# A Fourier layer's first pass over 64 images: another list of steps with the x transform in seven products, and DRAM chunk rows 72 KB apart

## The chip, the core and the metric

The kernel runs on one core of a Trainium2 chip. The metric is device time in microseconds from start to end of one execution. The core has a matrix engine (PE, with its weight loads shown apart as PEld), a vector engine (DVE), a scalar engine (ACT), a general engine (POOL), a queue engine that issues DMAs (SP), and 16 DMA engines between DRAM and the on-chip memory. PE writes its results into PSUM only, and ACT or DVE read them from there. Each engine works through its own instructions in order and waits on semaphores for the others.

## The reference, cut to what matters

Four Fourier layers run on 64 images of 256 x 256 points and 32 channels; then a small transformer block follows. Everything is fp32.

```python
v = transpose(concat([x, gx, gy]) @ p_w + p_b)        # 64 images, 32 channels, 256 x 256
for i in range(4):
    x_ft = rfft2(v)                                     # only 24 x 12 modes are used
    out_ft[:, :, :12, :12]  = einsum('bixy,ioxy->boxy', x_ft[:, :, :12, :12], W1[i])
    out_ft[:, :, -12:, :12] = einsum('bixy,ioxy->boxy', x_ft[:, :, -12:, :12], W2[i])
    v = irfft2(out_ft) + einsum('bcxy,cd->bdxy', v, w_w[i]) + w_b[i]
    v = (v - mean(v)) * rsqrt(var(v) + 1e-5) * bn_g[i] + bn_b[i]   # over batch and image
    if i < 3: v = relu(v)
h = concat([v @ q_w + q_b, txt])                        # 256 + 77 rows of 256 per image
h = h + attention(layernorm(h))
h = h + top_half_ffn(layernorm(h))
```

## The kernel before

**Stages.** The work of the Fourier layers is regrouped into passes over all images. `forward_first` takes the modes of the input, `mix` multiplies the modes by the layer's weights and yields the scale `s_` and shift `t_` of the normalization, and `layer(i, ...)` is one pass over the 64 images. It makes the activated image of layer i (inverse transform plus channel product, relu), writes it to DRAM for the next pass, and takes its forward transform and its sum of squares, which the next `mix` needs. There are three such passes (i = 0, 1, 2; "first", "second" and "third pass" here) and then the transformer stage, which reads the last image tensor (`ch<-v`).

**An image in a pass.** An image is cut into 8 chunks t. On chip a chunk is a tile `vo` of 128 partitions x 8 rows x 256 points; four `vo` buffers are used in turn. In DRAM an image is a tensor `vd`, 128 rows (partitions) of 8 chunks of 8 x 256 fp32, so one chunk of one row is 8 KB in one piece. There are two sets of 64 such tensors, which the passes read and write by turns.

**Steps.** The order of the work in a pass is a list of words written out by hand, `ORDER[0]` for the first pass and `ORDER[1]` for the second and third. The pass goes through the list once per image b; a word `name@n` acts on image b + n, and a suffix `.a` or `.d` picks ACT or DVE. What the words do, with the line that issues the work:

| word | engine | what it does |
|---|---|---|
| `lx`, `am`, `ld` | POOL, SP (and POOL), SP | load input rows (L649), load the mixed modes (L634) and scale them on POOL (L642), load a chunk of the last pass (L667, not in the first pass) |
| `sp`, `spT` | PE L673, DVE L681 | inverse transform over x for half an image; transpose it into tile `y` |
| `pre` t | PE L693 (and L704 after the first pass) | inverse transform over y plus channel product of chunk t |
| `evA`, `evB` | ACT L716 or DVE L718 | relu of one half of `pre` t from PSUM into `vo` |
| `st` t | SP L724, L728 | store chunk t to `vd`: in the first pass two DMAs of 512 KB, later one of 1 MB |
| `turn` t | DVE L733 | transpose chunk t into `t32` |
| `prod` t | PE L754 (L745 with `.w`) | channel product of chunk t for the next layer's squares |
| `sqA`, `sqB` | ACT L765 | square one half of it, with the sum kept |
| `y` k | PE L776 | forward transform over y, part k of 8, summed in PSUM |
| `half`, `zt0`, `zt1` | ACT L786, DVE L794 | move one half of the y result out of PSUM; transpose both into `zt` |
| `x`, `xe`, `xt`, `xo`, `xs` | PE, DVE or ACT, PE, ACT, SP | forward transform over x and its way to DRAM |

**The x transform has two forms.** The line `turned = "xt" in ORDER[min(i, 1)]` chooses. Where the list has no `xt`, as in the first pass before, `x` makes 12 products with the data stationary and the table of 96 columns moving (L819), and `xo` reads the result. Where it has `xt`, as in the second and third pass, `x` makes 4 products with the table `FX` stationary (64 columns) and 384 data columns moving (L808), `xe` copies the result out of PSUM (L831, L833), and `xt` makes 3 products that turn it and add its two halves (L838).

**The ring.** PSUM is cut into four slots of two banks. `pre`, `prod` and `y` take two slots each, `sp` and `x` one. A slot is taken in program order, always the one that has been free longest, and the step waits on the chip until whoever read the slot last is done:

```python
mine = sorted((k for k in range(4) if free[k] >= 0), key=lambda k: free[k])[:n]
```

A slot comes free (`close`) with `evA`/`evB` for `pre`, with `sqA`/`sqB` for `prod`, with `spT` for `sp`, with `zt0` and `half` for `y`, and with `xo` for `x`. While the eight `y` parts of one image are summed, two of the four slots are held, and everything else passes through the other two. Which slot a step gets thus follows from the list alone, and so does what each engine meets in which order.

**DMA queues.** All stores, chunk loads and `am` loads stand on SP's queue in the order of the list; `lx` and the scaling of `am` stand on POOL.

Of the kernel before, what the change touches and what calls it, by code (L numbers as in the profile page):

```python
# [9 lines left out]
F32 = mybir.dt.float32  # L10
# [6 lines left out]
S = 256  # L17
# [17 lines left out]
def _tables():  # L35
# [90 lines left out]


ORDER = [(
    "spT1 pre2 sqB1 lx0@1 evA2.a st1 evB2.d st2 pre3 evA3.d evB3.a prod0 y0@-1 sqB0 st0 "
    "sqA0 y1@-1 prod2 y2@-1 sqA2 turn0 am@2 sqB2 lx1@1 turn1 turn2 y3@-1 pre6 evB6.d "  # L130
    "y4@-1 y5@-1 evA6.a turn3 prod3 sqB3 y6@-1 y7@-1 sqA3 pre4 half.a@-1 st6 zt0@-1 lx2@1 "
    "evB4.a pre5 evA4.d prod4 evA5.a evB5.a turn4 sqA4 st3 sqB4 sp0@1 spT0@1 zt1@-1 turn5 "
    "st5 pre7 evB7.a lx3@1 evA7.a prod5 sqB5 prod6 sqA6 st4 x@-1 sqB6 turn6 sqA5 pre1@1 "
    "st7 xo@-1 pre0@1 evA1.a@1 evB1.d@1 evB0.a@1 xs@-2 evA0.d@1 prod7 sqB7 turn7 sqA7 "
    "prod1@1 sp1@1 sqA1@1 "
), (
    "evA2.a@1 evB2.a@1 ld5 ld7 pre4 ld0@1 turn6 prod6 evA4.a x@-1 evB4.d xe.d@-1 turn4 "
    "sqA6 sqB6 prod4 xt@-1 st2@1 turn2@1 sqA4 pre5 sqB4 xo@-1 am@2 evA5.d evB5.a pre3@1 "
# [15 lines left out]
def tile_fno_fusion_transformer(ctx: ExitStack, tc: tile.TileContext, a, cst_d, grid_d, out):  # L154
    nc = tc.nc
    x = a["x"].rearrange("b x y o -> b x (y o)")
    B = x.shape[0]
# [4 lines left out]
    dram = ctx.enter_context(tc.tile_pool(name="dram", bufs=1, space=DRAM))  # L162
# [19 lines left out]
    epsc = const.tile([128, 1], F32, name="epsc")  # L182
    nc.vector.memset(epsc, EPS)

    vd = [dram.tile([128, 8, 8, S], F32, name=f"v{b}_{n}") for n in range(2) for b in range(B)]
    vd = [vd[:B], vd[B:]]
    mix_d = [dram.tile([2, M, 2, B, 32 * C], F32, name=f"mix{i}") for i in range(L)]
    xh_d = [dram.tile([128, B, 144], F32, name=f"xh{i}") for i in range(1, L)]
# [1099 lines left out]
```

## Time and profile before

| what | value |
|---|---|
| median of 3 runs | 11210.26 us (11203.83 to 11220.63) |
| the profiled execution | 11214.0 us, of which span 11212.1 us, granted clock 0.984 |
| PE, PEld | 10666.4 us (95%), 5509.9 us (49%) |
| DVE, ACT, POOL | 8487.2 us (76%), 6483.7 us (58%), 1448.1 us (13%) |
| DMA | 3456.25 MB, mean 308 GB/s |
| `turn` on DVE (L733) | 1536 of 2292 ns |
| squares on ACT (L765) | 3072 of 1013 ns |
| evictions on ACT (L716), on DVE (L718) | 1792 of 1023 ns, 1280 of 1216 ns |
| x transform of the first pass (L819) | 1536 matmul records of 278 ns, from 264.6 to 2548.2 us |
| x transform of the second and third pass (L808, L838) | 1024 records of 499 ns, 768 of 281 ns; `xe` 128 of 557 ns |

The span is the time from the first to the last instruction on the core; the profiled execution is 1.9 us longer than its span. An fp32 product is recorded as two matmuls. A matmul's end is modelled, several run side by side in the array, and one that waits inside the array counts as busy: PE's 95% is therefore no measure of how full PE is, and its starts, in order of time, say more. "<-DMA v<-vo" after a time in brackets means that the engine stood idle for that time until a store had landed.

### The profile page before, as it was taken

What the parts mean: (1) busy time and instruction counts of PE and PEld (TensorE: products, weight loads), DVE (VectorE), ACT (ScalarE), POOL (GpSimd) and SP (SyncE); (2) the same over time, 40 slices, a digit from 0 to 9 for tenths busy, and PEclk for the clock granted to TensorE, in tenths of its full rate; (3) what the DMA queues carried; (4) which work ended last, traced back from release to release, by engine and by line L of the source; (5) the groups of instructions that cost most, each with busy time, mean ns of one, the idle gap of its engine ahead of it and who ended that gap; (6) DMA issues with size and microseconds to landing.
All of it is one profiled execution on the core that took longest, in us unless ns stands there. A gap on an engine that the chain in (4) does not pass through costs nothing. (4 is left out here: it accounts for less than half of the span.)

```text
span 11212.1 us, 395184 instructions
## 1 busy us (share of the span) xinstructions
PE 10666.4 (95%) x177174; PEld 5509.9 (49%) x177174; DVE 8487.2 (76%) x10525; ACT 6483.7 (58%) x10673; POOL 1448.1 (13%) x2179
## 2 busy tenths in 40 slices
PE   6999999997999999999799999999997999999999
PEld 3555555553444444444334444444443666666666
DVE  6888888887777777777777777777776666666665
ACT  5777777775665666666556566656663333333333
POOL 1111111110000000000000000000000333333333
PEclk8999999999999999999999999999998999999999
DMA  6767766678999999999899999999997555555553
GB/s 211 248 244 250 248 245 248 247 248 321 377 385 385 379 383 386 389 380 385 316 358 389 380 385 378 390 386 381 386 386 293 227 226 226 226 226 226 226 227 136
DMA packets 676795, 3456.25 MB, mean 308 GB/s; under 512 B 116248, under 2 KB 165784, under 8 KB 346008
## 3 DMA queue, kind: packets, MB, share of 16 engines
q1 hardware_dynamic: 609664, 3366.67, 76.6%
q0 software_dynamic: 58288, 60.60, 2.3%
q8 instruction: 1386, 22.71, 0.8%
q10 hardware_dynamic: 7144, 3.72, 0.1%
q14 instruction: 313, 2.56, 0.1%
HBM read 1733.60 MB, written 1696.92 MB: 306 GB/s over the span
## 5 line engine op out<-in xcount | busy, mean ns | idle before, releaser
L765 ACT ACTIVATE ring<-ring 128x1024 f32<-128x1024 f32 x3072 | 3112.4, 1013 | 1093.9 <-PE ring L745 612.9
L733 DVE STREAM_TRANSPOSE t<-vo 128x2048 f32<-128x2048 f32 x1536 | 3482.9, 2292 | 33.2 <-ACT vo L716 12.2
L716 ACT ACTIVATE vo<-ring 128x1024 f32<-128x1024 f32 x1792 | 1800.6, 1023 | 1584.1 <-PE ring L704 1264.5
L776 PE MATMUL ring<-t,cst 32*32 32x512 f32 x49152 | 1996.3, 599 | 34.5 <-issue 28.5
L754 PE MATMUL ring<-vo,w 32*32 32x512 f32 x40960 | 1898.8, 601 | 21.0 <-ACT vo L716 19.3
L718 DVE TENSOR_SCALAR vo<-ring 128x1024 f32<-128x1024 f32 x1280 | 1546.6, 1216 | 451.7 <-PE ring L704 276.5
L693 PE MATMUL ring<-cst,y 24*128 24x256 f32 x16384 | 1307.6, 404 | 89.3 <-ACT vo L716 45.5
L776 PEld LDWEIGHTS ring<-t,cst 32*32 32x32 f32 x49152 | 853.0, 103 | 979.5 <-issue 615.2
L642 POOL TENSOR_TENSOR ams<-ams,bns 48x512 f32<-48x512 f32 x384 | 401.1, 1044 | 6880.5 <-DMA ams<-mix 5410.8
L693 PEld LDWEIGHTS ring<-cst,y 24*128 24x128 f32 x16384 | 834.7, 185 | 922.5 <-ACT ring L765 246.5
L704 PE MATMUL ring<-vin,ws 32*32 32x512 f32 x32768 | 1196.2, 604 | 0.5 <-issue 0.5
L754 PEld LDWEIGHTS ring<-vo,w 32*32 32x32 f32 x40960 | 648.2, 103 | 845.5 <-issue 441.1
L681 DVE STREAM_TRANSPOSE y<-ring 128x1024 f32<-128x1024 f32 x384 | 761.2, 1982 | 341.4 <-PE ring L673 340.3
L794 DVE STREAM_TRANSPOSE zt<-ring 128x1024 f32<-128x1024 f32 x192 | 374.9, 1953 | 687.2 <-PE ring L776 687.2
L693 PE MATMUL ring<-mv,y 29*128 29x256 f32 x8192 | 704.2, 403 | 36.4 <-ACT ring L765 19.4
L693 PEld LDWEIGHTS ring<-mv,y 29*128 29x128 f32 x8192 | 455.8, 185 | 369.1 <-ACT ring L765 209.7
L1237 POOL DMA_DIRECT2D out_dram<-o x1024 | 511.3, 508 | 665.4 <-DVE o L1232 622.7
L765 ACT ACTIVATION_READ_ACCUMULATOR ring<-ring 128x1 f32 x3072 | 583.9, 190 | 0.0
L745 PE MATMUL ring<-vo,w 64*64 64x512 f32 x4096 | 506.8, 603 | 1.4 <-issue 1.4
L673 PE MATMUL ring<-ams,cst 49*128 49x512 f32 (+1 forms) x1536 | 452.0, 641 | 58.6 <-POOL ams L642 34.4
L1036 PE MATMUL hp<-ch,win 128*32 128x512 f32 x4096 | 471.9, 601 | 5.1 <-DMA ch<-v 5.1
L704 PEld LDWEIGHTS ring<-vin,ws 32*32 32x32 f32 x32768 | 249.1, 103 | 351.9 <-issue 350.9
(384 smaller groups left out, 10233.5 us busy)
## 6 DMA issues: line engine op xcount, KB each, us to landing
vin<-v SPq DMA_DIRECT2D x1024, 1024.0 KB, 10.3
v<-vo SPq DMA_DIRECT2D x1024, 1024.0 KB, 10.0
v<-vo SPq DMA_DIRECT2D x1024, 512.0 KB, 5.2
ch<-v SPq DMA_DIRECT2D x512, 1024.0 KB, 12.6
mix<-ob SPq DMA_DIRECT2D x48, 1024.0 KB, 4.9
ams<-mix SPq DMA_DIRECT2D x384, 96.0 KB, 8.7
xin<-in_x_dram SPq DMA_DIRECT2D x16, 1024.0 KB, 8.8
mv<-in_x_dram POOLq DMA_DIRECT2D x256, 64.0 KB, 7.7
```

Of the source, the lines that this page charges most:

```text
L681: nc.vector.transpose(y_[b, h].rearrange("p q c -> p c q"), ring[key][0][1].rearrange("p n (c k) -> p (n c) k", k=32),)
L693: nc.tensor.matmul(ps[n][:, 256 * r:256 * r + 256], lhsT=y_[b, t // 4][32 * n:32 * n + K, q:q + 4, :].rearrange("p q c -> p (q c)"), rhs=m ...
L704: nc.tensor.matmul(ps[n][32 * j:32 * j + 32], lhsT=ws[32 * n:32 * n + 32], rhs=v[32 * n:32 * n + 32, 2 * j:2 * j + 2, :], start=False, sto ...
L716: nc.scalar.activation(to, ring[key][h][1], AF.Relu)
L718: nc.vector.tensor_scalar(to, ring[key][h][1], 0.0, None, ALU.max)
L733: nc.vector.transpose(t32[b, t // 2][:, :, 8 * (t % 2):8 * (t % 2) + 8, :].rearrange("p y s c -> p s y c"), vo[b, t].rearrange("p s (y l) ...
L745: nc.tensor.matmul(ps[j][64 * m:64 * m + 64], lhsT=w64[64 * n:64 * n + 64], rhs=vo[b, t][64 * n:64 * n + 64, 2 * j:2 * j + 2, :], start=Tr ...
L754: nc.tensor.matmul(ps[n][32 * j:32 * j + 32], lhsT=w4[i + 1][32 * n:32 * n + 32], rhs=vo[b, t][32 * n:32 * n + 32, 2 * j:2 * j + 2, :], st ...
L765: nc.scalar.activation(ps, ps, AF.Square, accum_out=acc[:, at:at + 1])
L776: nc.tensor.matmul(ps[n][32 * j:32 * j + 32], lhsT=FYT[32 * n:32 * n + 32, k, :], rhs=t32[b, j][32 * n:32 * n + 32, k].rearrange("p s c -> ...
L1036: nc.tensor.matmul(hp[32 * g:32 * g + 32], lhsT=win[:, 7 - t:39 - t], rhs=ch[:, g], start=False, stop=t == 7, skip_group_check=True,)
L1237: nc.gpsimd.dma_start(out[b, 64 * n + 16 * g:64 * n + 16 * g + 16].rearrange("(p t) d -> p t d", t=2), o[32 * g + 8 * n:32 * g + 8 * n + 8 ...
```

## The change

The list of the first pass is replaced as a whole; it now has `xe.d` and `xt`, so the first pass takes its x transform in the second form (4 + 3 products). Per image the list still has 8 `pre`, 8 `prod`, 8 `y`, 8 `turn`, 16 squares and 16 evictions; of the evictions 11 are on ACT and 5 on DVE, where it was 10 and 6. More of image b + 1 is now done in the round of image b (`pre2`, `prod0`, `prod1` with their evictions and squares). The list of the second and third pass stays.

In DRAM each `vd` row gets a ninth chunk, which is never written or read: the 128 rows of an image lie 72 KB apart where they were 64 KB apart, for every store of the three passes, every chunk load of the second and third, and the loads of the transformer stage.

```diff
 ORDER = [(
-    "spT1 pre2 sqB1 lx0@1 evA2.a st1 evB2.d st2 pre3 evA3.d evB3.a prod0 y0@-1 sqB0 st0 "
-    "sqA0 y1@-1 prod2 y2@-1 sqA2 turn0 am@2 sqB2 lx1@1 turn1 turn2 y3@-1 pre6 evB6.d "
-    "y4@-1 y5@-1 evA6.a turn3 prod3 sqB3 y6@-1 y7@-1 sqA3 pre4 half.a@-1 st6 zt0@-1 lx2@1 "
-    "evB4.a pre5 evA4.d prod4 evA5.a evB5.a turn4 sqA4 st3 sqB4 sp0@1 spT0@1 zt1@-1 turn5 "
-    "st5 pre7 evB7.a lx3@1 evA7.a prod5 sqB5 prod6 sqA6 st4 x@-1 sqB6 turn6 sqA5 pre1@1 "
-    "st7 xo@-1 pre0@1 evA1.a@1 evB1.d@1 evB0.a@1 xs@-2 evA0.d@1 prod7 sqB7 turn7 sqA7 "
-    "prod1@1 sp1@1 sqA1@1 "
+    "y0@-1 st0 y1@-1 lx0@1 sqB1 turn0 turn1 st7@-1 sqA1 pre3 y2@-1 y3@-1 lx1@1 st2 evA3.a "
+    "turn2 y4@-1 evB3.a pre6 y5@-1 evB6.d lx2@1 evA6.a st1 turn3 prod2 y6@-1 sqA2 sqB2 "
+    "y7@-1 lx3@1 pre4 zt0@-1 half.a@-1 evA4.a turn6 st3 prod3 st6 evB4.a sp0@1 sqA3 pre5 "
+    "sqB3 spT0@1 evA5.a evB5.a st4 prod4 pre0@1 sqA4 zt1@-1 evB0.d@1 x@-1 xe.d@-1 sqB4 "
+    "turn4 evA0.a@1 prod6 sqA6 xt@-1 sqB6 prod5 xo@-1 sqB5 pre7 st5 sqA5 turn5 evA7.d "
+    "am@2 evB7.a pre1@1 prod0@1 evB1.d@1 evA1.a@1 sqA0@1 prod7 sqB0@1 sp1@1 xs@-2 sqB7 "
+    "turn7 sqA7 pre2@1 spT1@1 evB2.d@1 prod1@1 evA2.a@1 "
 ), (
...
-    vd = [dram.tile([128, 8, 8, S], F32, name=f"v{b}_{n}") for n in range(2) for b in range(B)]
+    vd = [dram.tile([128, 9, 8, S], F32, name=f"v{b}_{n}") for n in range(2) for b in range(B)]
```

## The prediction

> **What bounds it now.** I read the busy times by stage first, then one image of the first pass in order of time, engine by engine, then the waits. Columns of the stages: length, busy us of PE, weight loads, DVE, ACT, POOL, granted clock, DMA share, GB/s.
>
> ```profile
> 110.00:2460.00 2350.00, 2232.23 (x42548) 1175.85 (x42548) 2073.55 (x1270) 1761.89 (x2783) 282.39 (x387) 0.98 0.69 245
> 2700.00:5420.00 2720.00, 2668.18 (x53760) 1147.33 (x53754) 2084.51 (x1215) 1665.30 (x2616) 127.59 (x122) 1.00 0.97 383
> 5640.00:8440.00 2800.00, 2742.43 (x55340) 1180.20 (x55317) 2145.39 (x1249) 1711.85 (x2688) 129.64 (x124) 1.00 0.97 383
> 8600.00:11212.00 2612.00, 2516.92 (x15296) 1749.67 (x15296) 1733.79 (x6201) 967.42 (x1980) 847.42 (x1472) 0.99 0.56 219
> ```
>
> The reader sees four stages: first pass, second, third, transformer. PE looks full in all, but its ends are modelled; DMA is nearly full in passes two and three alone. The new list acts on the first line, the new pitch on all four. One image of the first pass (start, us, engine, line, record count; an fp32 product is two records, so x16 is one `pre`, x32 one `prod` or one `y`, x24 the x transform):
>
> ```profile
> 1472.34 2.01 PE L693 MATMUL ring<-mv,y 29*128 29x256 f32 x32
> 1474.60 2.58 PE L754 MATMUL ring<-vo,w 32*32 32x512 f32 x64 [0.25 <-ACT vo L716]
> 1477.37 1.13 PE L673 MATMUL ring<-ams,cst 54*128 54x512 f32 x4 [0.20 <-ACT ring L765]
> ...
> 1488.90 1.16 PE L693 MATMUL ring<-mv,y 29*128 29x256 f32 x16
> 1490.00 2.31 PE L776 MATMUL ring<-t,cst 32*32 32x512 f32 x62
> ...
> 1498.68 1.15 PE L754 MATMUL ring<-vo,w 32*32 32x512 f32 x32
> 1499.76 1.13 PE L673 MATMUL ring<-ams,cst 54*128 54x512 f32 x4
> 1500.82 1.64 PE L693 MATMUL ring<-mv,y 29*128 29x256 f32 x16
> 1502.39 3.76 PE L754 MATMUL ring<-vo,w 32*32 32x512 f32 x64
> 1506.08 2.92 PE L819 MATMUL ring<-cst,zt 128*128 128x96 f32 x24
> 1508.93 1.36 PE L693 MATMUL ring<-mv,y 29*128 29x256 f32 x20
> ```
>
> The cadence is 1508.93 - 1472.34 = 36.6 us. What PE must do in it: 8 `pre` at 1.0, 8 `prod` at 1.1, 8 `y` at 1.1, 2 `sp` at 1.06, x 2.85: 30.6 us. DVE: 8 `turn` at 2.2, 2 `spT` at 1.9, 2 `zt` at 1.96, 6 evictions at 1.17: 32.3 us. So no engine is full. The pass is bound by a **chain through the ring**: four PSUM slots, each filled by PE and emptied by ACT or DVE before the next step may write.
>
> From the rows in order of time I take: slot free to PE 0.1; `prod` start to its first square 1.3; square 1.03; `pre` start to eviction 1.18 on ACT, 1.24 on DVE; eviction 0.95 and 1.17; `y` 1.12; `sp` start to `spT` 1.2. The old chain, from `pre1` of one image to `pre1` of the next: pre1, evB1.d 2.41; prod7 1.4; sqB7 1.03; sp1 1.3; spT1 1.9; evB2.d, evA3.d 2.4; y0, y1 2.34; prod2 1.3; sqA2, sqB2 2.06; pre6 1.1; y4, y5, prod3, y6, y7 5.6; zt0 1.96; rest of pre5 0.9; evA5, evB5 1.9; sqA4, sqB4 2.06; evB7, evA7 1.9; prod6 1.2; x 2.85. Sum 35.6. The image above has 36.6, and one more wait:
>
> ```profile
> 1503.02 1.94 ACT L716 ACTIVATE vo<-ring 128x1024 f32<-128x1024 f32 x2 [0.71 <-DMA v<-vo]
> ```
>
> evB7 waits until the store of chunk 3 has left its `vo` buffer (issued at 1492.8, landed at 1502.9 by the trace's landing events). 36.6 - 0.7 = 35.9 against the sum 35.6: the chain is the right one. The mean cadence of the pass is 36.5 (starts of the `half` copy), so such waits cost some 0.65 per image.
>
> **The x transform, with the list.** Removed: 12 products with the data stationary, 2.85 us. Added: what passes two and three already do,
>
> ```profile
> 4238.24 1.51 PE L808 MATMUL ring<-zt,cst 128*64 128x384 f32 x8
> 4240.75 0.87 PE L838 MATMUL ring<-id,xe 128*128 128x48 f32 x6
> ```
>
> 1.44 + 0.80 = 2.24 on PE, and a DVE copy between (`xe`, 0.56). PE saves 0.6 per image. That is 64 x 0.6 = 39 us only if PE is the bound, and it is not; but x was the chain's last link, so what counts is the new chain. One eviction moves from DVE to ACT (DVE -1.17 + 0.56, ACT +0.95); DVE ends near 31.7 and ACT near 28 of 36: no bound.
>
> **The new list.** I gave every step the slot that `take` gives it (the longest free first) and followed the last wait back from `pre7` to `pre7`: sqB5, sqA5 2.06; evB7 0.95; prod0 1.4; sqA0 1.03; sp1 1.3; spT1 1.9; prod1 1.4; sqB1, sqA1 2.06; pre3 1.1; y2, y3, y4 3.36; pre6 to evB6.d 1.24; evB6.d 1.17; prod2 1.2; y6, y7 2.3; zt0 1.96; prod3 1.2; sp0 1.2; spT0 1.9; prod4 1.4; sqA4 1.03; x 1.54; prod6 1.3; sqA6 1.03; prod5 1.4. Sum 36.4, against 35.6 by the same prices: **+0.8 per image**. The shorter x and its split are eaten by both `spT` (1.9 each, sp0's now ahead of prod4) and by evB6 ahead of prod2 standing in the chain.
>
> Stores: on SP's queue the order is now st0, st7, st2, st1, st3, st6, st4, st5, then the two `am` loads and `xs`. st1 stands behind st2, which waits for evA2, the last step of the list. Each `vo` buffer (four, in turn) is needed again by the fourth `pre` after it; by the times of my chain a store then has at least 13.7 us from the moment SP may issue it (st1, needed by evA4), where st3, held behind st6, has 11.1 now (needed by evB7). So the 0.65 of store waits should shrink. Ends: all of it stays, or all of it goes. I take half, -0.33, since a landing took 10 us and slow packets in the DMA engines move with the list. Net +0.43 x 64 = +28 us. The x loads on POOL (`lx`), issued earlier, have over 20 us of cover before pre0; `am` moves from early to late in the image and is needed one image later, at sp0: both nothing.
>
> A rule that speaks against the list: the Trainium skill, "TensorEngine Tiling (Array Packing)", Key Properties, says that changing the tiling mode drains the array. The list goes from 13 changes of tile shape per image to 19. Row: a lone `pre` between others takes 1.1 (1488.90 to 1490.00), a pair 2.0 to 2.1, so a change there and back costs some 0.1, and six more 0.3 at most. My prices already stand in such places, so I add nothing; by the rule alone it would be up to +19 us, kept for the range.
>
> **The pitch.** A chunk row of 8 KB lies 72 KB from its neighbour, not 64; all transfers keep their sizes and counts. The skill's "DMA: Bandwidth & Descriptors", Latency and other measured facts, gives 207 GB/s per direction at a pitch of 512 KiB and 214 when padded: at most 3.3%, and nothing is stated at 64 KiB. Row: the trace's packets of 8 KB in passes two and three have a median of 309 ns (16 engines: 424 GB/s) and a mean of 328; the excess sits in two bursts of each image, one read of chunk 0 (496 ns) and the first packets after an idle queue, while the other chunks of the same pitch run at 310 to 315. A pitch that hurt would slow them all. By the row: 0. By the rule: DMA is 97% full in 5520 us, 3.3% is 182 us, at most 164, as the shortest image of these passes took 43.35 and the mean is 44.65. Below nothing: a new pitch with 2% slower packets would fill the DMA and cost some 110 us. I take 0. In the transformer the chunk loads hide behind PE (DMA share 0.56).
>
> **Sum**: 11214 (profiled execution, span 11212.1) + 28 = 11242; the runs shown have their median 4 us below it: **11238 us**, 0.25% slower. 0.2% (22 us) is about what a measurement can tell from no change.
>
> **Rivals.** *Store waits go wholly*: +0.8 - 0.65 = +0.15, +10 us: no change. For it: the slack of 13.7 us; against: landings spread. *PE decides*: the 0.6 counts in full, -39 us, 11171; for it PE's 95%, against it the 30.6 of 36.6. *The pitch pays*: half of 182 us, with the list's +28: 11150; for it DMA at 97% and evictions that wait for stores there, against it the 310 ns. *Slower still*: store waits stay and the drains count, (0.8 + 0.3) x 64 = +70, 11280; or the pitch costs 110: 11348. *The edit does nothing*: the pass tests the list for "xt", so the seven products do come.
>
> **Chances**: forecast 0.35, slower still 0.10, no change 0.24, PE decides 0.15, pitch pays 0.16. Slower 0.45, same 0.24, faster 0.31. The range 11120 to 11340 leaves out a pitch that pays or costs in full; the forecast's own is 11228 to 11270.
>
> **What will show it.** First-pass cadence 36.9 (36.5 before), with ACT's waits for `v` stores halved; zt0 still idle before y7; L808 and L838 at 1.44 and 0.80 in the first pass; passes two and three at 44.65 per image and 8 KB packets at 309 ns. Wrong if the cadence is under 36.3, or if passes two and three move by over 0.3 per image.

## The result, and the profile after

| | before | after |
|---|---|---|
| median, 8 runs each | 11203.66 us (11192.29 to 11220.63) | 11234.68 us (11222.58 to 11247.84) |
| ratio, 95% interval | 1 | 1.0024 [1.0015, 1.0032] |
| span of the profiled execution, granted clock | 11212.1 us, 0.984 | 11239.3 us, 0.982 |
| first pass, one `mix` to the next | 2442.6 us | 2488.5 us |
| second and third pass | 2978.2 and 2974.9 us | 2965.4 and 2969.9 us |
| from the last `mix` to the end | 2699.7 us | 2701.5 us |

The change costs 31 us by the medians, and 27 us by the ratio and by the two profiles. All of the loss is in the first pass, +46 us; before the first `mix` 3 us are saved, and the other two passes are 18 us shorter in this one profile (the second experiment shows what that is worth). The same four stages of the kernel after (length, busy us of PE, weight loads, DVE, ACT, POOL, granted clock, DMA share, GB/s):

```profile
110.00:2460.00 2350.00, 2146.29 (x41260) 933.13 (x41262) 2005.34 (x1248) 1782.56 (x2797) 277.18 (x377) 0.98 0.69 241
2700.00:5420.00 2720.00, 2671.23 (x53904) 1150.27 (x53904) 2092.97 (x1220) 1665.81 (x2615) 127.39 (x122) 1.00 0.97 385
5640.00:8440.00 2800.00, 2742.44 (x55258) 1180.68 (x55254) 2142.88 (x1248) 1708.88 (x2683) 129.49 (x124) 1.00 0.97 383
8600.00:11212.00 2612.00, 2512.98 (x15251) 1745.03 (x15252) 1735.39 (x6216) 963.49 (x1972) 835.29 (x1455) 0.99 0.57 222
```

In 2350 us of the first pass PE, the weight loads and DVE are less busy than before at the same granted clock (0.98), ACT a little more: x is shorter, one eviction went from DVE to ACT, and fewer images fit into the stretch. So the pass got longer with less work for PE. The other three lines are nearly those of before. One image of the first pass after, PE in order of time:

```profile
1442.47 1.15 PE L754 MATMUL ring<-vo,w 32*32 32x512 f32 x32 [0.75 <-DVE zt L794]
1443.56 1.13 PE L673 MATMUL ring<-ams,cst 54*128 54x512 f32 x4
...
1449.24 1.51 PE L808 MATMUL ring<-zt,cst 128*64 128x384 f32 x8 [0.27 <-ACT ring L765]
1450.68 1.14 PE L754 MATMUL ring<-vo,w 32*32 32x512 f32 x32
1451.75 0.87 PE L838 MATMUL ring<-id,xe 128*128 128x48 f32 x6
1452.55 1.78 PE L754 MATMUL ring<-vo,w 32*32 32x512 f32 x32
...
1455.71 0.70 PE L693 MATMUL ring<-mv,y 29*128 29x256 f32 x4 [0.20 <-ACT ring L765]
...
1459.19 1.15 PE L754 MATMUL ring<-vo,w 32*32 32x512 f32 x32 [0.25 <-DVE vo L718]
1460.31 1.13 PE L673 MATMUL ring<-ams,cst 54*128 54x512 f32 x4
...
1467.10 1.15 PE L693 MATMUL ring<-mv,y 29*128 29x256 f32 x16
1468.18 3.40 PE L776 MATMUL ring<-t,cst 32*32 32x512 f32 x96
1471.51 1.15 PE L693 MATMUL ring<-mv,y 29*128 29x256 f32 x16
...
1474.03 1.15 PE L754 MATMUL ring<-vo,w 32*32 32x512 f32 x32 [0.26 <-DVE vo L718]
...
1479.44 1.14 PE L754 MATMUL ring<-vo,w 32*32 32x512 f32 x30 [0.74 <-DVE zt L794]
```

From prod3 to prod3 it is 1479.44 - 1442.47 = 36.97 us. PE waits at places that the forecast's chain names: prod3 (the first and the last row) for zt0, x for sqA4, prod2 (1474.03) for evB6 on DVE. prod7 (1459.19) waits for evB1 on DVE as well; that is no link of the forecast's chain, which goes through sqA0 to sp1 there.

**A better measure than the mean.** The starts of the `half` copies give one cadence per image (61 of them). Their 10th percentile is taken for the cadence of the list when nothing disturbs it, and is called the floor from here on; the mean less the floor is the disturbance. e1 to e10 are the experiments of the next section. The last column names the x transform and the list, old as in before, new as in after; the pitch is 64 KB where no other is named.

| kernel | ratio to before, 95% interval | floor | median | mean | x form, list |
|---|---|---|---|---|---|
| before | 1 | 36.08 | 36.42 | 36.53 | old, old |
| after | 1.0024 [1.0015, 1.0032] | 36.97 | 36.98 | 37.15 | new, new, 72 KB |
| e1 | 1.0032 [1.002, 1.0044] | 36.97 | 36.99 | 37.14 | new, new |
| e2 | 0.9994 [0.9988, 1.0] | 36.08 | 36.44 | 36.54 | old, old, 72 KB |
| e3 | 1.0096 [1.0076, 1.0116] | 38.38 | 38.4 | 38.52 | old, new |
| e4 | 1.0047 [1.0031, 1.0062] | 36.55 | 37.0 | 37.2 | new, old |
| e5 | 1.0011 [1.0002, 1.0019] | 36.2 | 36.52 | 36.62 | new, old, `xt` before `pre1` |
| e6 | 1.0000 [0.9992, 1.0008] | 36.07 | 36.28 | 36.57 | old, old, `st3` early |
| e7 | 0.9990 [0.9982, 0.9999] | 36.07 | 36.33 | 36.49 | e6 with 72 KB |
| e8 | 1.0006 [0.9997, 1.0014] | 36.58 | 36.59 | 36.73 | new, new, `pre6` early |
| e9 | 1.0002 [0.9994, 1.001] | 36.59 | 36.6 | 36.68 | e8 with 72 KB |
| e10 | 1.0106 [1.0091, 1.0122] | 37.88 | 37.97 | 38.56 | e9, `y6`, `y7` before `prod2` |

So the floor grew by 36.97 - 36.08 = 0.89 per image, and the disturbance shrank from 0.45 to 0.18. Over the 62 intervals before the last image that is +39 us; the last image, from its predecessor's `half` to `mix`, takes 45.7 us instead of 40.4 (+5), and the start 139.8 instead of 137.9 (+2): the 46 us.

### The profile page after: what moved, and what is told of

It reads as the page before. It is cut to its first block, busy times and chain, and to the rows that moved or that the text cites. A ratio compares the mean times of both kernels' runs of the same rounds, so it can differ in the third digit from the quotient of the medians.

```text
span 11239.3 us, 394221 instructions
## 1 busy us (share of the span) xinstructions
PE 10623.4 (95%) x176534; PEld 5285.2 (47%) x176534; DVE 8452.6 (75%) x10525; ACT 6536.9 (58%) x10737; POOL 1445.8 (13%) x2179
## 5 line engine op out<-in xcount | busy, mean ns | idle before, releaser
L716 ACT ACTIVATE vo<-ring 128x1024 f32<-128x1024 f32 x1856 | 1858.1, 1022 | 1601.1 <-PE ring L704 1266.2
L776 PE MATMUL ring<-t,cst 32*32 32x512 f32 x49152 | 1908.6, 599 | 48.0 <-issue 30.4
L754 PE MATMUL ring<-vo,w 32*32 32x512 f32 x40960 | 1812.5, 601 | 79.4 <-DVE zt L794 46.3
L718 DVE TENSOR_SCALAR vo<-ring 128x1024 f32<-128x1024 f32 x1216 | 1478.2, 1216 | 533.4 <-PE ring L704 278.8
L776 PEld LDWEIGHTS ring<-t,cst 32*32 32x32 f32 x49152 | 785.9, 103 | 1014.1 <-issue 683.4
L754 PEld LDWEIGHTS ring<-vo,w 32*32 32x32 f32 x40960 | 564.9, 103 | 892.0 <-issue 408.0
```

The lines of the kernel that those rows point to most:

```text
L716: nc.scalar.activation(to, ring[key][h][1], AF.Relu)
L718: nc.vector.tensor_scalar(to, ring[key][h][1], 0.0, None, ALU.max)
L754: nc.tensor.matmul(ps[n][32 * j:32 * j + 32], lhsT=w4[i + 1][32 * n:32 * n + 32], rhs=vo[b, t][32 * n:32 * n + 32, 2 * j:2 * j + 2, :], st ...
L776: nc.tensor.matmul(ps[n][32 * j:32 * j + 32], lhsT=FYT[32 * n:32 * n + 32, k, :], rhs=t32[b, j][32 * n:32 * n + 32, k].rearrange("p s c -> ...
```

## The experiments

**e1 and e2: each half of the change alone.**

```diff
 e1: after, with the old pitch
-    vd = [dram.tile([128, 9, 8, S], F32, ...
+    vd = [dram.tile([128, 8, 8, S], F32, ...
 e2: before, with the new pitch
-    vd = [dram.tile([128, 8, 8, S], F32, ...
+    vd = [dram.tile([128, 9, 8, S], F32, ...
```

> The changed list with the 64 KB pitch of before. My theory (the list costs through its ring chain, the pitch nothing): first-pass cadence 37.0 to 37.2 us per image as in the changed kernel, passes two and three at 44.6 per image, time 11,230 to 11,240 (ratio 1.0024 to 1.0032). Rival (the pitch pays some 18 us in passes two and three, and hides part of the list's price, as the stage sums of one profile each might be read): 11,250, ratio 1.004. Rival (the pitch costs): ratio under 1.001.

> The old list with the 72 KB pitch. My theory: no change, ratio 0.9995 to 1.0005, with first-pass cadence 36.5 and 44.65 in passes two and three, the reads of chunk 0 still near 490 ns a packet. Rival (the pitch pays): 11,186, ratio 0.9984, cadence of passes two and three below 44.55. Rival (the pitch costs): ratio over 1.001.

The list alone is 0.32% slower and has the floor of after; the pitch alone leaves the first pass as it was. The loss is the list's. For the pitch there are four pairs that differ in nothing else: e2 to before -0.0006, after to e1 -0.0008, e7 to e6 -0.0010, e9 to e8 -0.0004. All have one sign and lie at the edge of what these runs can tell: at most about 0.1%, some 10 us, if anything. Single profiles don't show it: against its partner the second and third pass together are 47 us shorter in after and 14 us longer in e2, and the seven profiles with 64 KB spread over 5953 to 5992 us by themselves. The packets of 8 KB keep their median of 309 ns.

**e3: the new list with the old x transform** (against e1, pitch 64 KB).

```diff
-    ... evB0.d@1 x@-1 xe.d@-1 sqB4 ... sqA6 xt@-1 sqB6 prod5 xo@-1 ...
+    ... evB0.d@1 x@-1 sqB4 ... sqA6 sqB6 prod5 xo@-1 ...
```

> The changed list without its two words for the second form of the x transform, so the first pass has 12 products again; pitch 64 KB. Theory of the ring chain: x lies in the chain between sqA4 and prod6, so its 2.85 in place of 1.44 (xt and xe are off the chain) lengthens the cadence by 1.4 to 38.4, 11,235 + 62 x 1.4 = 11,320 (ratio 1.0105). Rival, PE's sum decides: 0.6 per image, cadence 37.6, 11,272 (ratio 1.006). Rival, x is hidden: cadence 37.0, 11,235.

The floor rises by 38.38 - 36.97 = 1.41, the length that x loses in the chain (2.85 - 1.44), and not by the 0.6 of PE's sum. In the new list x stands in the chain with its whole length; PE's 95% does not decide. The trace of e3 has x between the same neighbours as in after: prod4 (1449.65) and pre0 ahead of it, a wait for an ACT square, prod6 (1455.74) behind it:

```profile
1449.65 1.89 PE L754 MATMUL ring<-vo,w 32*32 32x512 f32 x32
1451.48 1.15 PE L693 MATMUL ring<-mv,y 29*128 29x256 f32 x16
1452.89 2.92 PE L819 MATMUL ring<-cst,zt 128*128 128x96 f32 x24 [0.27 <-ACT ring L765]
1455.74 2.11 PE L754 MATMUL ring<-vo,w 32*32 32x512 f32 x36
```

**e4 and e5: the old list with the new x transform.**

```diff
-    ... x@-1 sqB6 turn6 sqA5 pre1@1 ...
+    ... x@-1 sqB6 xe.d@-1 turn6 sqA5 pre1@1 xt@-1 ...      (e4)
+    ... x@-1 sqB6 xe.d@-1 turn6 sqA5 xt@-1 pre1@1 ...      (e5)
```

> The old list with the second form of the x transform put in (xe.d after sqB6, xt after pre1), pitch 64 KB: the x edit alone. Theory of the ring chain: pre1 no longer waits for x but for sqB6, 0.5 us earlier, yet evB1 on DVE then stands behind xe and turn6 and ends 0.3 later than before: cadence 36.5 to 36.9, 11,204 to 11,225 (ratio 1.000 to 1.002). Rival, PE's sum decides: 0.6 less per image, cadence 35.9, 11,165 (ratio 0.9965).

A miss for both theories. The trace of e4 in order of time, PE and ACT:

```profile
1494.02 0.87 PE L838 MATMUL ring<-id,xe 128*128 128x48 f32 x6
1494.82 1.57 PE L693 MATMUL ring<-mv,y 29*128 29x256 f32 x16
1494.92 0.28 ACT L845 COPY xo<-ring 128x144 f32<-128x144 f32 x1 [0.99 <-PE ring L838]
1495.10 1.03 ACT L716 ACTIVATE vo<-ring 128x1024 f32<-128x1024 f32 x1
```

xo stands on ACT ahead of the eviction of pre1. pre1 is finished, but ACT waits 0.99 for xt, which PE was to do after pre1; so evA1 and what follows come later. The wait recurs in every image (53.6 us in 54 waits between 400 and 2400 us). If that is why the mean cadence of e4 is 0.67 us above that of before, xt ahead of pre1 must remove the loss:

> The old list with the second x form as in oldlist_newx, but xt ahead of pre1 instead of behind it, so that xo on ACT, which stands ahead of evA1, no longer waits for pre1 and pre0's slot. If that wait of xo (1 us per image) made oldlist_newx slow, the cadence falls from 37.2 to 36.6 to 36.8, ratio 1.001 to 1.003. If the x form itself costs (more than the place of xt), it stays at 37.2, ratio 1.0047.

It removes most of it: the mean is 36.62, 0.58 lower, and the ratio 1.0011. Even so the shorter x gains nothing in the old list: with xe and xt behind it, the way from the start of x to that of xo is no shorter there (1512.04 to 1515.37 in e5, 3.33 us; 1506.08 to 1509.40 in before, 3.32).

**e6 and e7: fewer store waits in the old list.** The eviction of chunk 7 waits for the store of chunk 3, which stands behind st6 on SP's queue; here it is issued ahead of st6.

```diff
-    ... half.a@-1 st6 zt0@-1 ... turn4 sqA4 st3 sqB4 ...
+    ... half.a@-1 st3 st6 zt0@-1 ... turn4 sqA4 sqB4 ...
```

> The kernel before with one word moved: st3 stands before st6 on SP's queue (ahead of half), so the store of chunk 3 goes out once its data is there instead of behind evB6. Pitch 64 KB. My theory (0.65 us per image of the old list are waits for stores, most of them evB7 for st3): the waits of evB7 go, the first-pass cadence falls from 36.5 to 35.9 to 36.2, some 20 to 37 us less, ratio 0.9967 to 0.9982. Rival (the chain hides those waits, or another store becomes the late one): cadence 36.5, ratio 1.000.

> st3_early with the 72 KB pitch: if the pitch does nothing, the same ratio as st3_early within 0.0006; if it takes its 0.9994 again, 0.0006 lower.

My theory missed and its rival held. Waits for a store between 400 and 2400 us (total us, times, longest), first before, then e6:

```profile
ACT vo L716 <- DMA v<-vo: 25.9, 36, 2.0
DVE vo L718 <- DMA v<-vo: 4.6, 5, 1.4
```

```profile
ACT vo L716 <- DMA v<-vo: 9.9, 7, 1.6
DVE vo L718 <- DMA v<-vo: 4.5, 6, 0.9
```

Half of these waits are gone, and neither the mean cadence nor the time moves. The times decide here, since this one profile of e6 also has more of the stops shown below than that of before (20 against 11 of over 0.5 us): their interval leaves room for a gain of 9 us at most, where the waits taken away add to 16. So most of the disturbance of before is something else. Lining up the images of before event by event shows where its slow ones fall behind: in 24 of 55 images at evA6, together 14 us of some 23. In ten images pre6 itself is late, though y0 started on time. An undisturbed image of before, and one of the ten, PE:

```profile
1231.18 2.77 PE L776 MATMUL ring<-t,cst 32*32 32x512 f32 x62
1233.89 1.32 PE L693 MATMUL ring<-mv,y 29*128 29x256 f32 x16
...
1339.74 2.35 PE L776 MATMUL ring<-t,cst 32*32 32x512 f32 x38
1342.66 1.12 PE L776 MATMUL ring<-t,cst 32*32 32x512 f32 x24 [0.56 <-issue]
1343.71 1.15 PE L693 MATMUL ring<-mv,y 29*128 29x256 f32 x16
```

In the second, PE stops among the products of one step, waiting for nothing that the profile shows. Such stops account for 0.18 us per image of before (y0 to pre6 against its usual 5.73 us) and fall in the same images in e6. That is what neither theory had; the last section says what the stops have in common. e7, with this edit and the new pitch, is the fastest version found: 0.9990 [0.9982, 0.9999], just below before.

**e8 and e9: the end of y2 to y4 out of the new chain** (e8 against e1, e9 against after).

```diff
-    turn2 y4@-1 evB3.a pre6 y5@-1 evB6.d ...
+    turn2 evB3.a pre6 y4@-1 y5@-1 evB6.d ...
```

> The changed list with pre6 one y part earlier (before y4), pitch 64 KB. In the chain y2, y3, y4 stand between pre3 and pre6, while pre6's slots are free after y3. Theory of the ring chain: evB6 and prod2 come 0.3 earlier, cadence 36.7 against 37.0 to 37.1 with the same pitch, ratio to before 1.0015 to 1.002. Rival (that stretch is not in the chain): cadence unchanged, ratio 1.003.

The chain of the forecast goes pre3, y2, y3, y4, pre6. With y4 behind pre6 the floor falls by 36.97 - 36.58 = 0.39, where one y takes 1.1: y4 was in the chain, and after 0.39 another way must be as long; which one is open. The mean of 36.73 is the forecast's 36.7, and the ratio came out below the 1.0015 to 1.002 expected: the new list is then about as fast as before (1.0006 with an interval that holds 1).

> The new list with pre6 ahead of y4, and the rows 72 KB apart. By the chain the first pass keeps the 36.74 us per image that this list had with 64 KB; the pitch has taken 0.0006 to 0.0010 off in three pairs so far, each at the edge of its interval. Theory 'the pitch gives some 9 us in whatever list': ratio to before 0.9998 (0.9990 to 1.0003). Rival 'the three pairs were chance': 1.0006 again, as without the pitch. Either way passes two and three keep packets of 8 KB at a median of 309 ns.

1.0002 [0.9994, 1.001] lies between the two theories; it is the fourth pair above and settles nothing. No version of the new list beats before.

**e10: is the chain there y to zt0, or ACT?** (against e9)

```diff
-    ... turn3 prod2 y6@-1 sqA2 sqB2 y7@-1 lx3@1 pre4 ...
+    ... turn3 y6@-1 y7@-1 prod2 sqA2 sqB2 lx3@1 pre4 ...
```

> The same kernel with y6 and y7 ahead of prod2. In the trace DVE waits 1.9 us for y7 before zt0, and prod3 waits 0.74 us for zt0. Theory 'y7 to zt0 to prod3 is the chain there': y7 ends 1.1 us earlier, cadence 35.7 to 36.2, ratio 0.996 to 0.9995. Rival 'the chain goes by ACT': prod2 starts up to 2.2 us later, and sqA2, sqB2, half, evA4 and evB4 stand in one row on ACT ahead of sqA3, so all of them come later: cadence 37.5 to 38.8, ratio 1.004 to 1.012.

The rival holds. ACT and PE of e10 in order of time:

```profile
1447.47 1.78 PE L754 MATMUL ring<-vo,w 32*32 32x512 f32 x30
1450.32 0.70 PE L693 MATMUL ring<-mv,y 29*128 29x256 f32 x4 [1.07 <-ACT ring L765]
```

```profile
1449.15 1.01 ACT L765 ACTIVATE ring<-ring 128x1024 f32<-128x1024 f32 x1 [4.45 <-PE ring L754]
1450.17 1.02 ACT L765 ACTIVATE ring<-ring 128x1024 f32<-128x1024 f32 x1
1451.19 1.00 ACT L786 COPY half<-ring 128x1024 f32<-128x1024 f32 x1
1452.13 1.94 ACT L716 ACTIVATE vo<-ring 128x1024 f32<-128x1024 f32 x2
1453.95 1.03 ACT L765 ACTIVATE ring<-ring 128x1024 f32<-128x1024 f32 x1
```

ACT stands idle for 4.45 us until prod2 comes, and then has both squares, `half`, two evictions and the squares of prod3 in one row, while pre4 waits for the first of them. The wait of DVE before zt0 fell (from 1.92 us in e9 to 0.86) and bought nothing: an idle engine ahead of a step does not say that this step is the chain's.

## Why the prediction was right, step by step

- **A chain through the ring bounds the first pass, not PE**: shown. e3 moved the floor by x's 1.41, not by 0.6, and e8 by taking one link out; the other links are read from the traces, not each tested. "PE decides" (-39 us) is out.
- **Chain +0.8 per image**: +0.89. The links by the starts in the image of after: prod3 to x 6.77 (forecast 6.73), x to sp1 11.07 (10.71), sp1 to pre3 6.79 (6.66), pre3 to pre6 4.41 (4.46), pre6 to prod2 2.52 (2.41), prod2 to prod3 5.41 (5.46). The sum 36.4 was 0.54 short, most of it between x and sp1. There I took 0.1 from a free slot to PE, and the trace of after has 0.16 from the end of an ACT square (sqA4 starts at 1448.07 and takes 1.01, x starts at 1449.24) and 0.20 from the end of an ACT eviction (evB7 to prod0); only behind DVE is it less, 0.05 (zt0 to prod3). The old chain's 35.6 was short in the same way (36.08), so that the difference survived.
- **Store waits -0.33, half of 0.65**: the disturbance gave back 0.27, nearly that, but not as told. It was 0.45, not 0.65: I took the mean 36.53 less one image without its 0.71 of store wait (36.59 - 0.71 = 35.88), as if a wait cost its whole length. Against the floor of 36.08 that image was 0.51 longer, less than its wait, and I put all the rest of the mean down to stores. ACT's and DVE's waits for `v` stores were not halved in after; none is left between 400 and 2400 us. And e6 shows that they were not worth their length. A part of the 0.27 has another source: the profiles with the old list have 11 to 20 stops of PE of over 0.5 us between 200 and 2700 us, those with the new list 1 to 5 (last section). "Store waits go wholly" had the event right and its price wrong.
- **Net +0.43 per image**: 37.15 - 36.53 = 0.62. With the last image's 5 us, which the forecast left out, the first pass costs 46 us instead of 28. That the whole is nevertheless near +28 comes from the other passes, which were 18 us shorter in this profile, by chance or by the pitch. So much of the near hit is luck; the terms were further off than the total.
- **Drains taken at nothing**: the links explain the floor within their handovers, so there is no room for +0.3 (this is argued from the sums). No run varied the number of changes of tile shape alone.
- **Pitch 0**: between 0 and -0.1%, far from the rule's 164 us and from the rival, which took half of 182. The 214 GB/s behind that rule stands in the Trainium skill, "DMA: Bandwidth & Descriptors", Latency and other measured facts, for a padded pitch of 4 MiB, not of 512 KiB; no run here has either pitch. Passes two and three have a median of 44.55 and 44.47 per image (44.72 and 44.62 before), within the 0.3 given.
- **L808 and L838 at 1.44 and 0.80, DVE still idle before zt0**: x takes 1450.68 - 1449.24 = 1.44, and the next product starts 0.80 after xt; DVE's waits for y at zt0 add to 67.6 us in 54 images, where they were 108.8 in 55.

## What to carry to other kernels

Where steps share a few buffers in a hand-written order, write down the chain of handovers for the old and the new order by the same prices: their difference was good to 0.1 us here though each sum was half a microsecond short. Then compare the least disturbed images of both, and keep what disturbs them as a term of its own: a wait that has a name in the profile need not be worth its length, and a run that takes it away tells. A shorter operation pays with its whole length only where it is a link of that chain, and splitting it adds a link: put the second half ahead of whatever its reader's engine has waiting behind it.

## What was unexpected of the hardware

PE stops for 0.4 to 1.4 us in the middle of a row of independent products, with no wait in the profile, in one of some five images of before, at a granted clock of 1.00 in such a stretch of after (1612 to 1623 us). What the stops have in common is a place in PE's own program. The page of before has this DMA queue (packets, MB, share):

```profile
q8 instruction: 1386, 22.71, 0.8%
```

PE has 2 x 177,174 = 354,348 products and weight loads in that profile, so these 22.71 MB are 64 bytes for each of them; a packet is 22.71 MB / 1386 = 16.4 KB, which is then 256 instructions. Between 200 and 2700 us the twelve profiles have 106 stops of over 0.5 us between two products of one line for which the profile names no cause. With PE's records (products, weight loads and waits) numbered in order from 0, the product behind every one of these stops has a number that leaves 193 to 195 when divided by 256, and it starts 1.2 to 1.9 us after a packet of this queue has landed. In before the stop of 1342.66 is one: number 44,994, packet 1340.42 to 1341.35. So PE most likely waits there for its next instructions, which would also be why e6, whose order on PE is that of before, stops in the same images. No run varied this alone, so the cause is read from the traces and not tested.

In passes two and three the packets of 8 KB aren't slow by address: the read of chunk 7, which follows an idle queue, begins with packets of 591 and then 501 ns (means of eight in before) and comes down to 315 within its run, and the read of chunk 0, at a mean of 496 ns in before, took 313 in the first image of the pass, where it stands elsewhere in time. Over the twelve profiles, with either pitch, the mean of chunk 0 was 463 to 496.
